# Sixteen decoder entries on one core: eight in flight instead of seven, with fewer tiles for each

## The chip, the core and the metric

The kernel runs on one core of a Trainium2 chip. The core has four engines that compute: TensorE (PE in the profile, with its weight loads as PEld), VectorE (DVE), ScalarE (ACT) and GpSimd (POOL). SyncE (SP) issues most DMA transfers. Each engine works through its own list of instructions in order and waits on semaphores for the others. Products are written to PSUM, which has eight banks; everything else lies in SBUF. The metric is the time of one launch on the device in microseconds.

## What is computed

Sixteen independent entries (batch 16) of 128 tokens by 256 features pass through a decoder of two layers, all in float32. Each of the six blocks adds its output to x and normalises:

```
L0 attn : q,k,v = x W; q,k,v -> latents of 32; rotary; softmax (causal); back to 256; W
L0 xattn: linear attention with the context: q (k^T v); layer norm with gamma, beta
L0 ffn  : FP4 grid of x and of the weights; silu(gate) * up; FP4 grid again; down
L1 attn : softmax (causal) y, plus a moving part: sum_j qa.ka (x[j+1] - y[j]); W
L1 xattn: softmax with a mask over the context; W; norm; relu MLP 256-1024-256; norm
L1 ffn  : FP6 grid of x and of the weight; W + bias
```

In each attention there are 16 heads of 16 features. "FP4 grid" means that each block of 16 values is scaled by its largest and rounded to a grid of few values; FP6 has blocks of 32.

## The kernel before, in words

One entry fits the array: 128 tokens on the 128 partitions. An entry is written as a Python generator, `stages` (it calls `l0_attn` L837, `l0_xattn` L894, `l0_ffn` L985, `l1_attn` L1027, `l1_xattn` L1113 and `l1_ffn` L1176). Each `yield` names what the next step needs: the engine on which it starts, a resource ("p": one of four general PSUM banks; "quad": the one set of four banks for scores; "e": a pair of tiles for exponentials), and the tiles that it reads. Three more generators prepare weights: `fold_values` makes one matrix for the values of the first attention (resource "wv"), `later_biases` and `quantised_weights` (resource "gu").

A planner at the end of the kernel runs all generators when the program is built. It keeps its own clock for each engine, takes the step that can start first, and writes its instructions into the engines' lists. So the order of all instructions is fixed before the launch. Where several steps could start within 0.05 us of the first, it prefers one that holds a PSUM bank or another tile just written, then the one that became ready in the earliest interval of 8 us (each entry is shifted by its number in the table `DELAY`), then the oldest entry. `NS` (L18) entries are in flight. Entry b takes place b mod NS and starts when the entry before it in this place is done; the last place is given away only when the quantised weights are ready, since they are prepared in its tiles.

If the planner foresees that PE will wait at least `LEAST` us (L25), it fills the share `SHARE` of the gap with filler products (`fill`, L147; `ps_filler` in the profile), which nobody reads, as long as two of the general banks are free.

Every place owns tiles of SBUF, which `mine` (L252) gives out: A, B, C, D for intermediate results, v for values, mr for the mask's terms, yT for transposed features and results of 256 columns, and two tiles x0_ and x1_, between which x (`new_x`, L515) and the transposed input of the next entry (`load_input`, L278) take turns. A new use of a tile waits for all reads of the old one. `features` (L685) transposes a tile through PE and copies it with ACT into yT; `out_proj` (L691) multiplies, adds bias and residual, and writes the sum into yT. The tile bd, for the block diagonal in `l0_xattn`, is one for all entries.

The first attention computes scaled queries (`ps_qfk`, written to q in tile B) and then the values (`ps_v`). An attention takes scores in the quad (`ps_s`), their maxima on DVE (`nm`), splits them on POOL into three bfloat16 terms, transposes those on PE (`ps_tm`), computes transposed scores less the maxima (`ps_st`), exponentials on ACT (`e`), the causal zeros on POOL, the product with the values (`ps_yp`), and transposes that back (`ps_ty`). Masked parts of the score matrices and the small products of 16 features use 32-row groups of the array, all other products the whole array.

Of the kernel before, what the change touches and what calls it, by code (L numbers as in the profile page):

```python
# [16 lines left out]
P = 128  # L17
NS = 7  # L18
W3 = 3 * 4
# [4 lines left out]
EPS = 1e-5  # L24
SHARE, LEAST = 0.75, 0.8  # L25

DELAY = (3.07, 2.06, 3.48, 0.32, 3.35, 1.80, 2.92, 0.82, 1.65, 1.28, 1.58, 3.49, 2.27, 4.62, 2.80, 1.07, 0.06)
WINDOW = 3.413
# [185 lines left out]
def decoder_kernel(ctx: ExitStack, tc: tile.TileContext, a: dict, out: bass.AP):  # L214
# [12 lines left out]

    turns = {}

    def turn(name, n):  # L230
        turns[name] = turns.get(name, -1) + 1
        return turns[name] % n

    rings = {}
# [17 lines left out]
    def mine(s, tag, shape, name, dtype=F32):  # L252

        return ring(own, f"{tag}{s}", 1, shape, dtype, name)
# [23 lines left out]
    def load_input(b):  # L278

        s = b % NS  # L280
        t = mine(s, f"x{turn(f'x{s}', 2)}_", [P, 2, P], f"xT_in_{b}")
        nc.sync.dma_start(out=t, in_=a["xT"][:, :, b * T : (b + 1) * T])
        if b < 3:
            clock.load(t, 8 * P)
        else:
            arrives(t)
        incoming[b] = t
# [86 lines left out]
    for i in range(0, 5, 2):  # L374
        n = min(2, 5 - i)
        cm = wk.tile([P, 2, 64], F32, tag="bd", name="cm", bufs=1)
        GP.memset(cm, 0.0)
        GP.affine_select(
            out=cm, in_=cm, compare_op=ALU.is_ge, fill=-1e30, base=96 - 64 * i, pattern=[[-64, 2], [-1, 64]],
            channel_multiplier=1,  # L380
        )
        GP.tensor_copy(causal[:, i : i + n, :], cm[:, :n, :])
# [41 lines left out]
    clock.load(rows, 4 * (NROW - NADD))  # L424
    l2o = own.tile([P, H * VW], F32, tag="B5", name="l2o")
    nc.gpsimd.dma_start(out=l2o, in_=a["rows"][:, ROW["l2o"]].partition_broadcast(P))
# [17 lines left out]
    def bank(shape, name, dtype=F32):  # L444
        return psum(ps_p, "p", shape, name, dtype)
# [71 lines left out]
    def new_x(b, s, name):  # L517

        k = turn(f"x{s}", 2)
        return mine(s, f"x{k}_", [P, D], f"x_{name}_{b}")  # L520

# [162 lines left out]

    def features(y, s, name):  # L685

        yT = mine(s, "yT", [P, 2, P], f"yT_{name}")
        yield from transposed(y, 2, yT, name)
        return yT

    def out_proj(yT, weight, bias, residual, s, name):  # L691

        yield "PE", "p", yT
        p = bank((D,), f"op_{name}")
        product(p, yT, weight, bias)
        yield "V", p
        h = mine(s, "yT", [P, D], f"h_{name}")
        V.tensor_tensor(h, p, residual, ALU.add)
        return h
# [55 lines left out]
    def fold_values():  # L755
# [5 lines left out]
        yield "S", t  # L761
        vT = own.tile([P, 4, P], F32, tag="B4", name="fold_vT")
        S.copy(vT, t)
# [3 lines left out]
        yield "S", t  # L767
        kT = own.tile([P, P], F32, tag="D4", name="fold_kT")
        S.copy(kT, t)
# [4 lines left out]

        m = own.tile([P, 8 * VW], F32, tag="A4", name="fold_md")
        GP.memset(m, 0.0)
# [60 lines left out]
    def l0_attn(b, s):  # L837
# [12 lines left out]
        sin = w["sinT"].unsqueeze(1).to_broadcast([P, 4, P])  # L850
        q = mine(s, "B", [P, 4, P], f"q0_{b}")
        k = mine(s, "C", [P, 4, P], f"k0_{b}")
# [13 lines left out]
        for j, dst in ((0, rot), (2, k)):  # L866
# [5 lines left out]
            GP.tensor_tensor(dst, ro[0], ro[1], ALU.add)  # L872
        yield "PE", "p", rot
        p = bank((4, P), f"qfk_{b}")
        PE.matmul(p, lhsT=w["w_wqk"], rhs=rot, start=True, stop=True)
        yield "S", p
        S.activation(q, p, AF.Identity, bias=wqk_b, scale=LAT**-0.5)
        ctx_ = context(b, s, "0")
        yield "PE", "p", "wv", xT
# [3 lines left out]
        v = values(s, f"a0_{b}")  # L883
        S.copy(v[:, : H * VW], p)
        y = yield from attention(b, s, q, k, v, None, f"a0_{b}", "A")
        yield "PE", "bt", y
        yT = yield from features(y, s, f"a0_{b}")
        h = yield from out_proj(yT, w["w_cproj"], "cproj", xs[b], s, f"a0_{b}")
        xs[b] = new_x(b, s, "a0")
# [4 lines left out]
    def l0_xattn(b, s, ctx_):  # L894
        yield "PE", "p", ctx_
        p = bank((2 * D,), f"x0kv_{b}")
        product(p, ctx_, w["w_x0kv"], "x0kv")
        kv = mine(s, "A", [P, 2 * D], f"kv_{b}")
        yield "S", p
        S.copy(kv, p)  # L900
        xT = yield from features(xs[b], s, f"x0_{b}")
        yield "PE", "p2", kv, xT
        p2 = bank((2, P), f"x0m_{b}")
        for c in range(2):
            PE.matmul(
                p2[:, c, :], lhsT=kv[:, c * P : (c + 1) * P], rhs=kv[:, D + c * P : D + (c + 1) * P],
                start=True, stop=True,
            )
        p = bank((2, P), f"x0q_{b}")
        project(p, w["w_x0q"], xT)  # L910
        yield "S", p, p2
        qT = mine(s, "B", [P, 2, P], f"x0q_{b}")
        biased(qT, p, cols[:, COL["x0q"]])
        yield "V", "bd", p2
        bd = work("bd", 1, [P, 2, P], f"bd_{b}")
        V.tensor_tensor(bd, p2, w["blk"].unsqueeze(1).to_broadcast([P, 2, P]), ALU.mult)
        yield "PE", "p", bd, qT
        p3 = bank((2, P), f"x0a_{b}")
        for c in range(2):
            PE.matmul(p3[:, c, :], lhsT=qT[:, c, :], rhs=bd[:, c, :], start=True, stop=True)  # L920
        yield "V", p3
        h = mine(s, "yT", [P, D], f"h_x0_{b}")
        V.tensor_tensor(h, p3.rearrange("p a b -> p (a b)"), xs[b], ALU.add)
        xb = with_bias(b, s, "x0b", "A")
        z = mine(s, "C", [P, D], f"z_x0_{b}")
        yield from layernorm_affine(z, h, "x0g", xb, f"x0i_{b}")
        xs[b] = new_x(b, s, "x0")
        yield from layernorm(xs[b], z, f"x0_{b}")

# [55 lines left out]
    def l0_ffn(b, s):  # L985
        yield "V", "gu", xs[b]
        q = mine(s, "D", [P, D], f"xq_{b}")
        yield from fp4(q, xs[b], D, f"x_{b}")
        qT = yield from features(q, s, f"xq_{b}")
        h = mine(s, "A", [P, FF], f"hh_{b}")  # L990
# [29 lines left out]
        yield "V", p  # L1020
        r = mine(s, "yT", [P, D], f"h_f0_{b}")
        V.tensor_tensor(r, p, xs[b], ALU.add)
# [4 lines left out]
    def l1_attn(b, s):  # L1027
        xT = yield from features(xs[b], s, f"x1a_{b}")
        sc = HD**-0.5
        q = mine(s, "B", [P, 2, P], f"a1q_{b}")  # L1030
        k = mine(s, "C", [P, 4, P], f"a1k_{b}")
        qa = mine(s, "A", [P, 2, P], f"a1qa_{b}")
        ka = mine(s, "D", [P, 4, P], f"a1ka_{b}")
        yield "PE", "p", xT
# [9 lines left out]
        p = bank((2, P), f"a1k2_{b}")  # L1044
        project(p, w["w_a1k2"], xT)
        yield "S", p
        biased(ka[:, 2:4, :], p, dense_col("a1k2"), AF.Tanh, sc * 0.01)
# [9 lines left out]
        GP.tensor_copy(v3[:, :, :HD], xs[b].rearrange("p (h d) -> p h d", d=HD))  # L1057
        ahead = mine(s, "yT", [P, D], f"ahead_{b}")
        nc.sync.dma_start(out=ahead[: P - 1, :], in_=xs[b][1:P, :])
# [44 lines left out]
        yield "S", p  # L1104
        yT = mine(s, "yT", [P, 2, P], f"yT_a1_{b}")
        S.copy(yT, p)
        h = yield from out_proj(yT, w["w_a1p"], "a1p", xs[b], s, f"a1_{b}")
        xs[b] = new_x(b, s, "a1")
# [4 lines left out]
    def l1_xattn(b, s, ctx_):  # L1113
# [24 lines left out]
        S.copy(v[:, : H * VW], p)  # L1138
        xT = yield from features(xs[b], s, f"x1_{b}")
        yield "PE", "p", xT  # L1140
# [4 lines left out]
        y = yield from attention(b, s, q, k, v, mr, f"x1_{b}", "A")  # L1145
        yT = yield from features(y, s, f"x1y_{b}")
        h = yield from out_proj(yT, w["w_x1o"], "x1o", xs[b], s, f"x1_{b}")
        t = mine(s, "C", [P, D], f"x1_{b}")
        yield from layernorm_affine(t, h, "g1", row("be1"), f"x1i_{b}")
        tT = yield from features(t, s, f"x1t_{b}")  # L1150
        ff = []
# [15 lines left out]
        yield "V", p  # L1167
        h = mine(s, "yT", [P, D], f"h_ff_{b}")
        V.tensor_tensor(h, p, t, ALU.add)
# [6 lines left out]
    def l1_ffn(b, s):  # L1176
# [4 lines left out]
        yield from fp6(q, xs[b], D, f"f1_{b}")  # L1181
        qT = yield from features(q, s, f"f1_{b}")
        h = yield from out_proj(qT, wf, "f1", xs[b], s, f"f1_{b}")
        y = mine(s, "C", [P, D], f"out_{b}")
# [14 lines left out]
    places = {"quad": ("s", 1), "p": ("p", 1), "p2": ("p", 2), "t2": ("t2", 1), "t22": ("t2", 2)}  # L1199
    places.update((tag, (tag, 1)) for tag in ("fc", "fC", "silu", "bd", "mT", "mi", "mb"))  # L1200
    free = {"e": [0.0, 0.0], "mx": [0.0, 0.0], "gu": [], "wv": [], "bt": []}
# [79 lines left out]
    while runs:  # L1281
# [3 lines left out]


        at, _, run = min(
            (r for r in able if r[0] <= first + 0.05),
            key=lambda r: (not r[2].held, round((r[2].ready + DELAY[int(r[1]) if r[1] >= 0 else B]) / 8.0), r[1]),
        )  # L1290
        run.step(at)
# [118 lines left out]
```

## Time and profile before

| | us |
|---|---|
| median of three runs | 985.59 (984.91 to 986.45) |
| the profiled execution, its own time | 988.3 |
| its span, first to last instruction | 986.6 |
| PE busy | 919.7 |
| of it fillers (182) | 44.5 |
| PEld busy | 723.2 |
| DVE busy | 700.7 |
| ACT busy | 508.8 |
| POOL busy | 432.2 |

The mean granted clock of TensorE is 0.983 of full speed. The DMA engines are nearly idle after the first 50 us. Since almost all operations pass through one helper, nearly every line in the profile is L208 and operations are told apart by their tiles. A name such as `ps_op_a` is that of a PSUM tile: op for output product, the suffix for the block (a: an attention, x: a cross attention, f: a feed-forward block). Busy times of PE are modelled at their ends and include short stalls between pipelined products.

### The profile page before, as it was taken

The numbers are of one execution on the slowest core, as the hardware profiler recorded it, in microseconds if no ns is written. First come the engines' busy times: TensorE is split into PE (matmuls) and PEld (weight loads), VectorE is DVE, ScalarE is ACT, GpSimd is POOL, SyncE is SP. The second block draws the span as 40 slices with busy tenths as digits, with TensorE's granted clock in tenths as the row PEclk, the third lists the DMA queues.
The fourth block names the chain that finished last, engine by engine and source line by source line (L and its number), as shares of the span: only waits on it lengthen the run. The fifth ranks groups of instructions, "written<-read, shape, count | busy, mean of one in ns | idle before, by whom it ended". The sixth has DMA issues, their size and how long they took to land.

```text
span 986.6 us, 28364 instructions
## 1 busy us (share of the span) xinstructions
PE 919.7 (93%) x11965; PEld 723.2 (73%) x11965; DVE 700.7 (71%) x1440; ACT 508.8 (52%) x1113; POOL 432.2 (44%) x898
## 2 busy tenths in 40 slices
PE   7889899999899999999999999999998899999996
PEld 6566567777678878788777787878776687686764
DVE  5999999976764666659596967957666458963544
ACT  3244445665556444655546666555555545555432
POOL 3335523644435344445363464435434435344321
PEclk9899999999999989999999999999999999999998
DMA  8910000000000000000000000000000000000000
GB/s 230 210 45 7 28 7 7 11 9 20 5 23 12 19 25 21 23 22 17 18 18 16 21 13 7 24 1 23 21 13 25 8 11 7 14 13 15 10 7 12
DMA packets 47864, 25.57 MB, mean 26 GB/s; under 512 B 23004, under 2 KB 45516, under 8 KB 47480
## 3 DMA queue, kind: packets, MB, share of 16 engines
q1 hardware_dynamic: 46816, 22.39, 8.3%
q8 instruction: 94, 1.54, 0.6%
q0 software_dynamic: 192, 0.93, 0.4%
q10 hardware_dynamic: 728, 0.44, 0.1%
q14 instruction: 34, 0.28, 0.1%
HBM read 19.57 MB, written 2.10 MB: 22 GB/s over the span
## 4 chain that ended last, share of the span: by engine, by line
PE 55%; DVE 26%; ACT 8%; POOL 6%; issue 4%; DMA 0%; ACTq 0%; POOLq 0%; DVEq 0%
PE ps_ff L208 10%; PE ps_s_a L208 3%; PE ps_dn L208 3%; PE ps_st_a L208 3%; DVE nm_a L208 3%; DVE rope L208 2%; PE ps_op_a L208 2%; PE ps_x0kv L208 2%; PE ps_pg L208 2%; PE ps_pu L208 2%; PE ps_a1qk L208 2%; PE ps_yt L208 2%; DVE hh L208 2%; PE ps_qk L208 2%; PE ps_st_x L208 2%
## 5 line engine op out<-in xcount | busy, mean ns | idle before, releaser
L208 POOL TENSOR_SCALAR_AFFINE_SELECT e_a<-e_a 128x1024 f32<-128x1024 f32 x64 | 76.0, 1190 | 88.9 <-ACT e_a L208 88.7
L208 DVE TENSOR_REDUCE nm_a<-ps_s_a 128x16 f32<-128x2048 f32 x32 | 73.1, 2286 | 28.4 <-PE ps_s_a L208 28.2
L208 ACT ACTIVATE e_a<-ps_st_a 128x1024 f32<-128x1024 f32 x64 | 65.7, 1030 | 27.1 <-PE ps_st_a L208 26.9
L208 PE MATMUL ps_ff<-yT_x1t,w 128*128 128x128 f32 x512 | 63.1, 277 | 1.0 <-ACT yT_x1t L208 1.0
L208 PEld LDWEIGHTS ps_ff<-yT_x1t,w 128*128 128x128 f32 x512 | 60.1, 192 | 4.4 <-issue 2.1
L208 PE MATMUL ps_ff<-w,ff 128*128 128x256 f32 x256 | 61.0, 381 | 0.0
L208 ACT ACT_TABLE_LOAD x41 | 52.6, 1283 | 12.8 <-DMA brow<-in_rows_dram 9.0
L208 POOL CAST maxima<-nm_a 128x16 bf16<-128x16 f32 x32 | 8.9, 279 | 98.8 <-DVE nm_a L208 98.8
L208 PEld LDWEIGHTS ps_ff<-w,ff 128*128 128x128 f32 x256 | 46.2, 190 | 7.7 <-ACT ff L208 1.0
L208 ACT ACTIVATE ff<-ps_ff,cols 128x128 f32<-128x128 f32 x128 | 36.5, 369 | 27.1 <-PE ps_ff L208 27.0
L208 PE MATMUL ps_dn<-qw_down,hT 128*128 128x256 f32 x192 | 47.2, 383 | 0.7 <-ACT hT L208 0.5
L208 PE MATMUL ps_pg<-gu,yT_xq 128*128 128x352 f32 x128 | 44.7, 471 | 0.7 <-DVE hh L208 0.4
L208 DVE TENSOR_REDUCE nm_x<-ps_s_x 128x16 f32<-128x2048 f32 x16 | 36.5, 2282 | 11.4 <-PE ps_s_x L208 11.1
L161 PE MATMUL ps_filler<-ones,ident_b 128*128 128x512 bf16 x182 | 44.5, 383 | 0.0
L208 PE MATMUL ps_pu<-gu,yT_xq 128*128 128x352 f32 x128 | 43.2, 460 | 0.6 <-DVE bd L208 0.6
L208 PE MATMUL ps_yp_a<-e_a,v_a 128*32 128x128 f32 x1024 | 36.5, 281 | 3.6 <-POOL e_a L208 2.3
L208 ACT ACTIVATE e_x<-ps_st_x 128x1024 f32<-128x1024 f32 x32 | 31.8, 1026 | 13.7 <-PE ps_st_x L208 13.7
L208 PEld LDWEIGHTS ps_dn<-qw_down,hT 128*128 128x128 f32 x192 | 34.4, 190 | 5.6 <-ACT hT L208 0.7
L208 POOL TENSOR_SCALAR_AFFINE_SELECT maT<-maT 128x1024 f32<-128x1024 f32 x16 | 18.0, 1123 | 42.0 <-ACT maT L208 42.0
L208 ACT ACTIVATE x_x<-z_x,rstd_x 128x256 f32<-128x256 f32 x32 | 19.3, 604 | 31.7 <-POOL rstd_x L208 26.8
L208 ACT ACTIVATE x_a<-h_a,rstd_a 128x256 f32<-128x256 f32 x32 | 19.4, 605 | 31.4 <-POOL rstd_a L208 29.9
L208 PEld LDWEIGHTS ps_yp_a<-e_a,v_a 128*32 128x32 f32 x1024 | 26.3, 111 | 12.0 <-issue 4.8
(367 smaller groups left out, 2659.2 us busy)
## 6 DMA issues: line engine op xcount, KB each, us to landing
ctx<-in_ctxT_dram SPq DMA_DIRECT2D x32, 128.0 KB
xT_in<-in_xT_dram SPq DMA_DIRECT2D x16, 128.0 KB
w<-in_w_dram SPq DMA_DIRECT2D x2, 1024.0 KB
x_in<-in_x_dram SPq DMA_DIRECT2D x16, 128.0 KB
out_dram<-out SPq DMA_DIRECT2D x16, 128.0 KB
ahead<-x_f SPq DMA_DIRECT2D x16, 127.0 KB
mi<-in_mask_dram SPq DMA_DIRECT2D x16, 64.0 KB
rows<-in_rows_dram POOLq DMA_DIRECT2D x1, 768.0 KB, 5.5
```

What stands on the lines that cost most here:

```text
L161: self._e.matmul(bank, lhsT=lhsT, rhs=rhs, start=True, stop=True)
L208: return f(*args, **kw)
```

## The change

- Eight entries are in flight (`NS` 8). Sixteen entries are so two rounds.
- To make room, each place loses yT and one of its two x tiles. What went to yT goes to one of A, B, C, D whose content the entry has done with; the place is now an argument of `features` and `out_proj`. x has one tile, x, written in place by each norm. The next entry's transposed input goes to B. bd goes to the entry's own D. The row-shifted x ("ahead") shares tile A with the rectified queries qa.
- In the first attention the values' product stands ahead of the scaled queries, since the transposed input lies in B, where the queries go.
- The planner's rule is shorter: of the steps that can start first, without the margin of 0.05 us, the one that became ready first, then the oldest entry. `DELAY` and the preference for held tiles go. `LEAST` is 1.0 instead of 0.8 us.
- In the preparation, some tiles of places 4 and 5 are taken from other tiles or places.

```
-NS = 7
+NS = 8
-SHARE, LEAST = 0.75, 0.8
-
-DELAY = (3.07, 2.06, 3.48, 0.32, 3.35, 1.80, 2.92, 0.82, 1.65, 1.28, 1.58, 3.49, 2.27, 4.62, 2.80, 1.07, 0.06)
+SHARE, LEAST = 0.75, 1.0
...
-        t = mine(s, f"x{turn(f'x{s}', 2)}_", [P, 2, P], f"xT_in_{b}")
+        t = mine(s, "B", [P, 2, P], f"xT_in_{b}")
...
-        k = turn(f"x{s}", 2)
-        return mine(s, f"x{k}_", [P, D], f"x_{name}_{b}")
+        return mine(s, "x", [P, D], f"x_{name}_{b}")
...
-    def features(y, s, name):
+    def features(y, s, at, name):
 
-        yT = mine(s, "yT", [P, 2, P], f"yT_{name}")
+        yT = mine(s, at, [P, 2, P], f"yT_{name}")
...
-    def out_proj(yT, weight, bias, residual, s, name):
+    def out_proj(yT, weight, bias, residual, s, at, name):
...
-        h = mine(s, "yT", [P, D], f"h_{name}")
+        h = mine(s, at, [P, D], f"h_{name}")
...
-        yield "PE", "p", rot
-        p = bank((4, P), f"qfk_{b}")
-        PE.matmul(p, lhsT=w["w_wqk"], rhs=rot, start=True, stop=True)
-        yield "S", p
-        S.activation(q, p, AF.Identity, bias=wqk_b, scale=LAT**-0.5)
-        ctx_ = context(b, s, "0")
         yield "PE", "p", "wv", xT
         p = bank((H * VW,), f"v0_{b}")
         product(p, xT, wv, "l2o")
         yield "S", p
         v = values(s, f"a0_{b}")
         S.copy(v[:, : H * VW], p)
+        yield "PE", "p", rot
+        p = bank((4, P), f"qfk_{b}")
+        PE.matmul(p, lhsT=w["w_wqk"], rhs=rot, start=True, stop=True)
+        q = mine(s, "B", [P, 4, P], f"q0_{b}")
+        ctx_ = context(b, s, "0")
+        yield "S", p
+        S.activation(q, p, AF.Identity, bias=wqk_b, scale=LAT**-0.5)
...
-        yield "V", "bd", p2
-        bd = work("bd", 1, [P, 2, P], f"bd_{b}")
+        yield "V", p2
+        bd = mine(s, "D", [P, 2, P], f"bd_{b}")
...
-        qa = mine(s, "A", [P, 2, P], f"a1qa_{b}")
-        ka = mine(s, "D", [P, 4, P], f"a1ka_{b}")
+        both = mine(s, "A", [P, 4, P], f"a1qa_{b}")
+        qa, ahead = both[:, 0:2, :], both[:, 2:4, :].rearrange("p a b -> p (a b)")
...
-
-        at, _, run = min(
-            (r for r in able if r[0] <= first + 0.05),
-            key=lambda r: (not r[2].held, round((r[2].ready + DELAY[int(r[1]) if r[1] >= 0 else B]) / 8.0), r[1]),
-        )
+        at, _, run = min((r for r in able if r[0] <= first), key=lambda r: (r[2].ready, r[1]))
```

More of the change, by code (lines that the diff above doesn't have):

```diff
@@ L226, in decoder_kernel @@
     ps_p = ctx.enter_context(tc.tile_pool(name="ps_p", bufs=4, space=bass.MemoryType.PSUM))
[L228 to L232, printed above, removed]
     rings = {}
@@ L375, in decoder_kernel @@
         n = min(2, 5 - i)
-        cm = wk.tile([P, 2, 64], F32, tag="bd", name="cm", bufs=1)
+        cm = wk.tile([P, 2, 64], F32, tag="mb", name="cm", bufs=2)
         GP.memset(cm, 0.0)
@@ L424, in decoder_kernel @@
     clock.load(rows, 4 * (NROW - NADD))
-    l2o = own.tile([P, H * VW], F32, tag="B5", name="l2o")
+    l2o = own.tile([P, H * VW], F32, tag="D5", name="l2o")
     nc.gpsimd.dma_start(out=l2o, in_=a["rows"][:, ROW["l2o"]].partition_broadcast(P))
@@ L761, in fold_values @@
         yield "S", t
-        vT = own.tile([P, 4, P], F32, tag="B4", name="fold_vT")
+        vT = own.tile([P, 4, P], F32, tag="C6", name="fold_vT")
         S.copy(vT, t)
@@ L767, in fold_values @@
         yield "S", t
-        kT = own.tile([P, P], F32, tag="D4", name="fold_kT")
+        kT = own.tile([P, P], F32, tag="D6", name="fold_kT")
         S.copy(kT, t)
@@ L773, in fold_values @@
         yield "S", p
-        m = own.tile([P, 8 * VW], F32, tag="A4", name="fold_md")
+        m = own.tile([P, 8 * VW], F32, tag="A6", name="fold_md")
         GP.memset(m, 0.0)
@@ L850, in l0_attn @@
         sin = w["sinT"].unsqueeze(1).to_broadcast([P, 4, P])
-        q = mine(s, "B", [P, 4, P], f"q0_{b}")
         k = mine(s, "C", [P, 4, P], f"k0_{b}")
@@ L884, in l0_attn @@
         S.copy(v[:, : H * VW], p)
+        yield "PE", "p", rot
[5 more added lines that the diff above has]
+        S.activation(q, p, AF.Identity, bias=wqk_b, scale=LAT**-0.5)
         y = yield from attention(b, s, q, k, v, None, f"a0_{b}", "A")
         yield "PE", "bt", y
-        yT = yield from features(y, s, f"a0_{b}")
-        h = yield from out_proj(yT, w["w_cproj"], "cproj", xs[b], s, f"a0_{b}")
+        yT = yield from features(y, s, "B", f"a0_{b}")
+        h = yield from out_proj(yT, w["w_cproj"], "cproj", xs[b], s, "C", f"a0_{b}")
         xs[b] = new_x(b, s, "a0")
@@ L900, in l0_xattn @@
         S.copy(kv, p)
-        xT = yield from features(xs[b], s, f"x0_{b}")
+        xT = yield from features(xs[b], s, "C", f"x0_{b}")
         yield "PE", "p2", kv, xT
@@ L921, in l0_xattn @@
         yield "V", p3
-        h = mine(s, "yT", [P, D], f"h_x0_{b}")
+        h = mine(s, "C", [P, D], f"h_x0_{b}")
         V.tensor_tensor(h, p3.rearrange("p a b -> p (a b)"), xs[b], ALU.add)
         xb = with_bias(b, s, "x0b", "A")
-        z = mine(s, "C", [P, D], f"z_x0_{b}")
+        z = mine(s, "D", [P, D], f"z_x0_{b}")
         yield from layernorm_affine(z, h, "x0g", xb, f"x0i_{b}")
@@ L988, in l0_ffn @@
         yield from fp4(q, xs[b], D, f"x_{b}")
-        qT = yield from features(q, s, f"xq_{b}")
+        qT = yield from features(q, s, "B", f"xq_{b}")
         h = mine(s, "A", [P, FF], f"hh_{b}")
@@ L1020, in l0_ffn @@
         yield "V", p
-        r = mine(s, "yT", [P, D], f"h_f0_{b}")
+        r = mine(s, "D", [P, D], f"h_f0_{b}")
         V.tensor_tensor(r, p, xs[b], ALU.add)
@@ L1027, in l1_attn @@
     def l1_attn(b, s):
-        xT = yield from features(xs[b], s, f"x1a_{b}")
+        xT = yield from features(xs[b], s, "D", f"x1a_{b}")
         sc = HD**-0.5
@@ L1045, in l1_attn @@
         project(p, w["w_a1k2"], xT)
+        ka = mine(s, "D", [P, 4, P], f"a1ka_{b}")
         yield "S", p
@@ L1057, in l1_attn @@
         GP.tensor_copy(v3[:, :, :HD], xs[b].rearrange("p (h d) -> p h d", d=HD))
-        ahead = mine(s, "yT", [P, D], f"ahead_{b}")
         nc.sync.dma_start(out=ahead[: P - 1, :], in_=xs[b][1:P, :])
@@ L1104, in l1_attn @@
         yield "S", p
-        yT = mine(s, "yT", [P, 2, P], f"yT_a1_{b}")
+        yT = mine(s, "A", [P, 2, P], f"yT_a1_{b}")
         S.copy(yT, p)
-        h = yield from out_proj(yT, w["w_a1p"], "a1p", xs[b], s, f"a1_{b}")
+        h = yield from out_proj(yT, w["w_a1p"], "a1p", xs[b], s, "B", f"a1_{b}")
         xs[b] = new_x(b, s, "a1")
@@ L1138, in l1_xattn @@
         S.copy(v[:, : H * VW], p)
-        xT = yield from features(xs[b], s, f"x1_{b}")
+        xT = yield from features(xs[b], s, "A", f"x1_{b}")
         yield "PE", "p", xT
@@ L1145, in l1_xattn @@
         y = yield from attention(b, s, q, k, v, mr, f"x1_{b}", "A")
-        yT = yield from features(y, s, f"x1y_{b}")
-        h = yield from out_proj(yT, w["w_x1o"], "x1o", xs[b], s, f"x1_{b}")
+        yT = yield from features(y, s, "B", f"x1y_{b}")
+        h = yield from out_proj(yT, w["w_x1o"], "x1o", xs[b], s, "D", f"x1_{b}")
         t = mine(s, "C", [P, D], f"x1_{b}")
         yield from layernorm_affine(t, h, "g1", row("be1"), f"x1i_{b}")
-        tT = yield from features(t, s, f"x1t_{b}")
+        tT = yield from features(t, s, "B", f"x1t_{b}")
         ff = []
@@ L1167, in l1_xattn @@
         yield "V", p
-        h = mine(s, "yT", [P, D], f"h_ff_{b}")
+        h = mine(s, "A", [P, D], f"h_ff_{b}")
         V.tensor_tensor(h, p, t, ALU.add)
@@ L1181, in l1_ffn @@
         yield from fp6(q, xs[b], D, f"f1_{b}")
-        qT = yield from features(q, s, f"f1_{b}")
-        h = yield from out_proj(qT, wf, "f1", xs[b], s, f"f1_{b}")
+        qT = yield from features(q, s, "A", f"f1_{b}")
+        h = yield from out_proj(qT, wf, "f1", xs[b], s, "D", f"f1_{b}")
         y = mine(s, "C", [P, D], f"out_{b}")
@@ L1199, in decoder_kernel @@
     places = {"quad": ("s", 1), "p": ("p", 1), "p2": ("p", 2), "t2": ("t2", 1), "t22": ("t2", 2)}
-    places.update((tag, (tag, 1)) for tag in ("fc", "fC", "silu", "bd", "mT", "mi", "mb"))
+    places.update((tag, (tag, 1)) for tag in ("fc", "fC", "silu", "mT", "mi", "mb"))
     free = {"e": [0.0, 0.0], "mx": [0.0, 0.0], "gu": [], "wv": [], "bt": []}
```

## The prediction

> **What bounds the kernel now.** I read the page's busy shares and its 40 slices first.
>
> ```profile
> PE 919.7 (93%) x11965; PEld 723.2 (73%) x11965; DVE 700.7 (71%) x1440; ACT 508.8 (52%) x1113; POOL 432.2 (44%) x898
> ...
> PE   7889899999899999999999999999998899999996
> ...
> PEclk9899999999999989999999999999999999999998
> ```
>
> TensorE is the bound: 93%, and no other engine over 71%. But part of its work is fillers, products that nobody reads. So I took the stretches next, for all instructions and then for the fillers alone.
>
> ```profile
> 0.00:200.00 200.00, 178.22 (x2212) 131.57 (x2212) 179.60 (x364) 85.72 (x193) 88.00 (x179) 0.97 0.26 67
> 200.00:880.00 680.00, 649.99 (x8671) 523.56 (x8659) 473.07 (x973) 379.98 (x825) 310.42 (x641) 0.99 0.06 16
> 880.00:986.60 106.60, 91.48 (x1094) 68.06 (x1094) 48.06 (x105) 43.12 (x97) 33.77 (x80) 0.97 0.04 12
> ```
>
> ```profile
> 0.00:200.00 200.00, 17.87 (x71) 0.97 0.26 67
> 200.00:880.00 680.00, 6.82 (x27) 0.99 0.06 16
> 880.00:986.60 106.60, 19.78 (x84) 0.97 0.04 12
> ```
>
> Columns: stretch, length, then busy us of PE, PEld, DVE, ACT, POOL (in the second view PE's fillers alone), clock, DMA. Useful PE work is busy less fillers: 643.2 us of 680 in the middle (94.6%), 71.7 of 106.6 in the tail (67%). The first 200 us are DVE's (179.6), quantising weights. The tail's timeline shows the loss itself:
>
> ```profile
> 956.42 2.97 PE L161 MATMUL ps_filler<-ones,ident_b 128*128 128x512 bf16 x13
> ...
> 969.29 6.64 PE L161 MATMUL ps_filler<-ones,ident_b 128*128 128x512 bf16 x30
> 978.55 0.41 PE L208 MATMUL ps_tr_f<-ident,f1q 128*128 128x128 f32 x2 [2.62 <-DVE f1q L208]
> ```
>
> From 969.29 on PE only waits for the last entry's layer norm and FP6 grid, fillers or not. The third loss is the clock, here around 348 us:
>
> ```profile
> 346.10:349.50 3.40, 1.61 (x11) 0.95 (x14) 3.26 (x6) 1.81 (x4) 2.93 (x6) 1.00 0.05 15
> 349.50:352.90 3.40, 3.40 (x54) 2.89 (x55) 2.20 (x4) 0.72 (x2) 2.14 (x3) 0.50 0.06 19
> 352.90:356.30 3.40, 3.40 (x40) 2.45 (x43) 1.03 (x3) 1.59 (x2) 0.43 (x2) 0.50 0.03 8
> ```
>
> A window in which PE is about half busy is followed by one or two at half clock. The middle has four such windows (one at 236.9, two here, one at 752.3): 4 x 3.4 us at half speed, 6.8 us of work lost.
>
> **The change, part by part.** No instruction of the computation is added or removed; the order is new. I compared the two orders of PE instructions as the programs write them.
>
> *Fillers.* 182 before, 97 after. Up to the same point of the work, about 200 us: 71 before, 69 after. In the middle 27 before, none after. In the tail 84 before, 28 after (4 and 24, ahead of the last two entries' FP6 transposes). The planner fills three quarters of a gap it foresees, so it foresees no gap of 1 us or more in the middle. The raised threshold explains little: only two of the 28 groups before have two fillers, the size that it forbids.
>
> *The tail.* With 7 in flight, 16 entries run as 7, 7 and 2: the last 180 of 6978 product instructions before belong to entries 14 and 15 alone. In the new order, 8 and 8, entries 11 to 15 are all in those 180. What stays is the last chain: 17.3 us (986.6 - 969.29), six fillers fewer (6 x 0.221 = 1.3; 30 took 6.64), plus the gap of 4 fillers (4 x 0.221 / 0.75 = 1.2): 17.2 us, with 1.6 of useful work in it. The other 70.1 us (71.7 - 1.6) now run like the middle.
>
> *The middle's share p.* Taking out the 27 fillers alone gives 643.2 / (680 - 6.8) = 95.5%. I also take back half of the clock loss, 3.4 us, since no large gap is foreseen: 643.2 / 669.8 = 96.0%. Bounds are from the 100 us stretches, fillers out: the best is 600 to 700 (98.19 - 0.81 = 97.4%), the worst 700 to 800 (92.30 - 1.46 = 90.8%). I lean to the upper half because dependent steps lie farther apart. I summed the PE work that the order puts between two steps of one entry, at the spacing of such products in the trace. Medians: values' product to its transposes in the last attention 1.9 us before, 4.2 after; transposed maxima to the second scores there 2.4 and 9.8; scores to maxima 4.8 and 7.8. Before, the 1.9 us are just enough: at 948.32 that product starts, and its transposes at 951.22 without idle time behind one step of another entry.
>
> *Dearer switches of the array's mode.* Between row groups and the full array I count 373 changes before, 392 after. Starts of full-array products follow each other in 112 ns; across a change 200 to 309 ns. So 19 x about 0.145 = 2.7 us (1.7 to 3.7).
>
> The page "TensorEngine Tiling (Array Packing)", section Key Properties, says that a change of tiling mode, though not of tile, drains TensorE; this speaks against an order that alternates more. It gives no price; the spacings above are such a drain, and a sum by the rule alone could not be made.
>
> *Values' product ahead of scaled queries.* Attention now waits for one more PE step and one ACT step behind the values: ps_qfk 0.59 x 2 passes, overlapping to 1.0, and ACT q 0.69. Later seven other entries cover it; for the first entry, behind the folded weights, I take 1.0 (0 to 1.7). The copy of the values is ahead of q on ACT now; nobody but this entry waits.
>
> *Tiles.* One x tile: the layer norm's write (0.60 us on ACT) must follow all reads of the old x, of which only "ahead", the DMA of x moved one row, is not on the entry's own chain. It is issued before the attention that precedes the write, ten steps earlier; the output's subtraction waits for it in both kernels. Bounds 0 to 0.7 (its issue takes 670 ns) a time, I take 0. It now lands in the second half of the tile that holds the rectified queries, whose reader, the masked product, comes after attention: 0. The next entry's xT goes to tile B and is issued at the same place, its x after the place is free: x is read only at the first residual, some 1000 PE instructions later. Features and results in tiles A to D replace yT; each overwrites what an earlier step of the same chain has read: 0. Tile bd, one for all before, becomes the entry's own, which can only free DVE (0.4 us each): 0. POOL's bias sum xb_be (0.85 us) now has to follow the reads of t's transposed copy, done before the ACT step that precedes it: 0. On SP's queue the contexts' loads wait for PE as before (111.9 us behind ps_qfk, off the path); what stands behind them is loads for much later. If that cover went, a load would cost its whole landing to one entry of eight, not to PE.
>
> *ACT.* 31 table loads instead of 41, 1.28 us each: 12.8 us of an engine that is 52% busy; 0, bounds -1 and 0.
>
> **Sum.** Start 200 - 0.5 (two fillers) = 199.5; modes and queries 3.7; useful work of middle and tail 643.2 + 70.1 = 713.3 at share p; end 17.2. So time = 220.4 + 713.3 / p. At p = 96.0%: 220.4 + 743.0 = 963.4 against the profiled span of 986.6, that is -23.2. The profiled run took 988.3, the median of the three runs shown is 985.6, 1.0 below the span; so 962.4, say 962.
>
> The skill's first page, "Trainium Kernel Development and Optimization", section Performance Expectations, calls matmul busy time a poor measure because products are pipelined, and points to weight-load busy. By that measure the tail's useful loads are 68.06 - 8.01 = 60.1 us, about 58.7 before the last chain, at the middle's (523.56 - 2.48) / 680 = 76.6%: 76.6 us instead of the 73.0 that 70.1 takes at 96.0%, so 966 by it. The rule also makes the 96% less of a ceiling than it looks.
>
> **Rivals.**
>
> A. *The middle stays or gets a little worse.* New stalls of under 1 us, which get no filler, take the freed time; a first-ready rule also lets started steps hold PSUM banks longer, and with fewer than two of four free no filler is put in, so missing fillers don't prove missing gaps. For it: 200 to 300 us had 90.6% useful (93.72 - 3.13), seven points below the best stretch. Against: the longer covers. At 94.6%: 974.4 - 1.0 = 973; it spans p from 95.3% to 93.4%, 968 to 983.
>
> B. *Slower: bank starvation in the middle.* Eight entries queue for the four general PSUM banks and the one quad of score banks; PE stops until ACT or DVE has read a bank, windows fall to half busy, and the clock halves after them. It decides from p = 93.1% down (713.3 / 0.931 = 766.2, and 766.2 + 220.4 = 986.6). Two of seven middle stretches lie below that already; at the worst one's 90.8% the time is 1005. Against: the stretches from 300 to 500 ran seven entries at 97%.
>
> C. *Much better.* Busy shares hide small stalls, and longer covers remove them and all four slow windows. At 97.4%: 952.7 - 1.0 = 952; at the best stretch's whole busy share, 98.2%, 946.
>
> D. *The tail's gain is not real:* the last five entries collide on DVE (FP6 grid, some 4 us each with norms) and the tail stays at 67%. That gives back 70.1 / 0.67 - 73.0 = 32 us, 994. Against: DVE is 45% busy in the tail (48.06 of 106.6). I put it with B.
>
> **How the numbers follow.** Forecast, p 95.3 to 96.8%, 956 to 968: 0.49. A: 0.23. C: 0.13. B and D: 0.12. Within 0.2% (2 us), about what a measurement of this kernel tells from no change: 0.03. Faster: 0.49 + 0.23 + 0.13 = 0.85. The range leaves out B and D, and the lower half of C: 947 to 983.
>
> **What would show it.** Right: ps_filler x97, none between 200 and 930 us; 880 us to the end over 80% useful; useful share of the middle 95.3% or more; clock mean above 0.983; the last filler group of 24 followed by one FP6 transpose. Wrong: PE waits for ACT or DVE copies growing in the middle, with half-clock windows there; a share under 93.1%; a first pair of gate and up products much later than 127 us, which would mean that first-ready order delays the weights.

## The result, and the profile after

The changed kernel takes 969.87 us (median of four runs, 968.28 to 972.29) against 986.02 before: a ratio of 0.984, 95% interval 0.982 to 0.986. It is 1.6% faster. The prediction said 962 with a range of 947 to 983. The profiled execution took 968.28, its span is 966.2, which stands against 963.4 in the prediction's sum.

The page of the changed kernel, busy shares and slices:

```profile
PE 896.6 (93%) x11880; PEld 715.2 (74%) x11880; DVE 699.8 (72%) x1440; ACT 491.4 (51%) x1103; POOL 437.1 (45%) x898
...
PE   7888899888999999999999999999998899999996
...
PEclk9998999999999999999999999999999999999998
```

The share of PE is again 93%, though the time fell: a share of busy time alone would not have shown the gain. The stretches do, first all instructions, then the fillers alone (columns as in the prediction: stretch, length, busy us of PE, PEld, DVE, ACT, POOL, clock, DMA):

```profile
0.00:200.00 200.00, 167.82 (x2140) 122.51 (x2140) 163.77 (x320) 82.47 (x177) 80.86 (x158) 0.95 0.27 69
200.00:880.00 680.00, 653.47 (x8991) 531.00 (x8992) 482.48 (x976) 372.18 (x833) 325.61 (x668) 1.00 0.06 16
880.00:966.20 86.20, 75.30 (x751) 61.67 (x749) 53.54 (x145) 36.70 (x95) 30.68 (x73) 0.95 0.03 11
```

```profile
0.00:200.00 200.00, 16.59 (x69) 0.95 0.27 69
200.00:880.00 680.00, 0.00 (x0) 1.00 0.06 16
880.00:966.20 86.20, 6.37 (x28) 0.95 0.03 11
```

Busy less fillers, the useful work, is 151.2 us in the first 200 us (before: 160.3), 653.5 of 680 in the middle, 96.1% (before 94.6%), and 68.9 of 86.2 in the tail, 80% (before 67%). So the middle and the tail gained, and the start lost 9.1 us. The tail in time order:

```profile
946.57 1.03 PE L159 MATMUL ps_filler<-ones,ident_b 128*128 128x512 bf16 x4
947.80 0.44 PE L206 MATMUL ps_tr_f<-ident,f1q 128*128 128x128 f32 x2 [0.21 <-DVE f1q L206]
...
949.67 5.34 PE L159 MATMUL ps_filler<-ones,ident_b 128*128 128x512 bf16 x24
957.10 0.56 PE L206 MATMUL ps_tr_f<-ident,f1q 128*128 128x128 f32 x2 [2.09 <-DVE f1q L206]
```

On PE only the last entry's chain is left then, 16.5 us from 949.67 to the end. Six entries write their results after 880 us (from 901.26 to 962.84), before four (from 883.89 to 983.26). Between 200 us and that point PE does this:

```profile
200.00:949.67 749.67, 720.58 (x9710) 588.94 (x9710) 530.02 (x1103) 406.30 (x923) 353.10 (x732) 1.00 0.05 15
949.67:966.20 16.53, 8.19 (x32) 3.73 (x30) 5.99 (x18) 2.59 (x5) 3.18 (x9) 0.73 0.05 16
```

With the four fillers (0.9 us) out, that is 719.7 / 749.67 = 96.0% useful.

### The profile page after: what moved, and what is told of

Same layout as the page of the kernel before. It is cut to its first block, busy times and chain, and to the rows that moved or that the text cites. A ratio compares the mean times of both kernels' runs of the same rounds, so it can differ in the third digit from the quotient of the medians.

```text
span 966.2 us, 28159 instructions
## 1 busy us (share of the span) xinstructions
PE 896.6 (93%) x11880; PEld 715.2 (74%) x11880; DVE 699.8 (72%) x1440; ACT 491.4 (51%) x1103; POOL 437.1 (45%) x898
## 5 line engine op out<-in xcount | busy, mean ns | idle before, releaser
L206 POOL TENSOR_SCALAR_AFFINE_SELECT e_a<-e_a 128x1024 f32<-128x1024 f32 x64 | 76.6, 1197 | 55.1 <-ACT e_a L206 54.9
L206 POOL CAST maxima<-nm_a 128x16 bf16<-128x16 f32 x32 | 10.8, 336 | 89.6 <-DVE nm_a L206 89.6
L206 POOL TENSOR_TENSOR rot<-rope,rope 128x512 f32<-128x512 f32 x16 | 21.6, 1350 | 37.1 <-DVE rope L206 35.2
L206 PE MATMUL ps_qk<-xT_in,w_qkv 128*128 128x128 f32 x256 | 36.1, 305 | 1.3 <-DMA xT_in<-in_xT_dram 0.7
L206 PEld LDWEIGHTS ps_qk<-xT_in,w_qkv 128*128 128x128 f32 x256 | 34.6, 218 | 2.6 <-ACT yT_x L206 0.9
L206 POOL TENSOR_TENSOR k<-rope,rope 128x512 f32<-128x512 f32 x16 | 21.9, 1368 | 29.6 <-DVE rope L206 29.6
## 6 DMA issues: line engine op xcount, KB each, us to landing
a1qa<-x_f SPq DMA_DIRECT2D x16, 127.0 KB
```

What stands on the lines that cost most here:

```text
L206: return f(*args, **kw)
```

## The experiments

Twelve kernels were run, each in three rounds beside the kernel before on the same chip; ratios are to that. The parts of the change form a table: entries in flight, tiles (with the values' place), and the planner's rule. "Table" is the shift `DELAY`, whose numbers are those of the kernel before in every row that has it. Start is useful PE work in the first 200 us, middle the useful share from 200 to 880 us.

| kernel | in flight | tiles | rule | median us | ratio (95%) | start us | middle |
|---|---|---|---|---|---|---|---|
| before | 7 | old | old, table | 986.0 | 1 | 160.3 | 94.6% |
| e11 | 7 | old | old, no table | 1006.90 | 1.022 (1.018 to 1.026) | 154.0 | 92.5% |
| e2 | 7 | old | new | 1028.57 | 1.045 (1.042 to 1.047) | 155.0 | 93.2% |
| e10 | 7 | new | old, table | 1019.17 | 1.034 (1.031 to 1.036) | 153.3 | 91.2% |
| e12 | 7 | new | old, no table | 1015.84 | 1.030 (1.027 to 1.034) | 156.4 | 93.0% |
| e3 | 7 | new | new | 1016.28 | 1.032 (1.030 to 1.035) | 155.6 | 94.2% |
| e1 | 8 | new | old, table | 979.72 | 0.995 (0.993 to 0.997) | 157.0 | 95.5% |
| after | 8 | new | new | 969.87 | 0.984 (0.982 to 0.986) | 151.2 | 96.1% |
| e4 | 8 | new, queries first | new | 963.90 | 0.978 (0.975 to 0.981) | 153.0 | 95.9% |
| e5 | 8 | new | old in preparation, then new | 959.12 | 0.974 (0.970 to 0.977) | 159.5 | 96.2% |
| e6 | 8 | new, queries first | as e5 | 979.28 | 0.993 (0.990 to 0.995) | 154.2 | 94.1% |
| e7 | 8 | new, no fillers | new | 977.12 | 0.991 (0.988 to 0.993) | 158.3 | 95.4% |
| e13 | 8 | new | as e5, margin kept | 956.02 | 0.968 (0.964 to 0.972) | 158.6 | 96.7% |
| e14 | 8 | new | as e5, 4 us intervals | 961.06 | 0.975 (0.972 to 0.978) | 158.6 | 95.8% |

### One part alone, or one undone

The first four asked which part makes the gain and which the loss at the start. The rule alone, on the kernel before:

```
-            (r for r in able if r[0] <= first + 0.05),
-            key=lambda r: (not r[2].held, round((r[2].ready + DELAY[...]) / 8.0), r[1]),
+        at, _, run = min((r for r in able if r[0] <= first), key=lambda r: (r[2].ready, r[1]))
```

> The kernel before with only the planner's rule of the change (first able, then first ready; fillers from 1.0 us), seven in flight, all tiles as before. Theory 1, the gain is the eighth entry: no gain here; the order writes 228 fillers instead of 182, 46 more at 0.244 us, so about 986 + 11 = 997 us, with the tail after 880 us still under 70% useful. Rival 2, the gain is the shorter rule: 975 us or less.

It took 1028.57 us, 4.5% slower: theory 1 in direction, but four times the 11 us that its fillers foretold. Then the changed kernel with one entry fewer:

```
-NS = 8
+NS = 7
-        vT = own.tile([P, 4, P], F32, tag="C6", name="fold_vT")
+        vT = own.tile([P, 4, P], F32, tag="C4", name="fold_vT")
(kT and m likewise)
```

> The changed kernel with seven entries in flight instead of eight; tiles, values ahead of queries and rule as changed (three tiles of the preparation go to place 4). Theory 1: the gain is lost, 222 fillers instead of 97, 125 more at 0.244 us, 970 + 30 = 1000 us, between 990 and 1005. Rival 2, rule or tiles give the gain: 975 us or less. Against e2 it prices the tiles and the values' place alone: theory 1 expects less than 4 us between the two.

1016.28 us, 11 above theory 1's range. This run and the changed kernel differ in the number of entries alone (beside the places of three preparation tiles), so under these tiles and this rule the eighth entry is worth 46.4 us. The same step under the old rule with its table (e10 to e1 below, which differ in the filler threshold too) is worth about 39 us, so it is not the luck of one pair of orders. Its stretches and fillers show where the time goes:

```profile
200.00:880.00 680.00, 650.97 (x8836) 527.82 (x8838) 460.38 (x943) 367.66 (x818) 306.73 (x644) 0.99 0.06 16
880.00:1014.90 134.90, 109.31 (x1097) 76.19 (x1094) 65.16 (x149) 47.61 (x107) 38.01 (x87) 0.98 0.03 10
```

```profile
200.00:880.00 680.00, 10.22 (x42) 0.99 0.06 16
880.00:1014.90 134.90, 27.41 (x117) 0.98 0.03 10
```

The tail is 48.7 us longer than the changed kernel's, with 81.9 useful us in 134.9 (61%). The last three results are written at 900.66, 1003.51 and 1011.52, so for 114 us only two entries are left (before: for 49 us, from 937.37 on). The middle is at 94.2% instead of 96.1%. The other prediction in this expectation failed: e2 and e3 differ by 12 us, not by less than 4, and the new tiles are on the faster side.

The changed kernel with the old rule:

```
-        at, _, run = min((r for r in able if r[0] <= first), key=lambda r: (r[2].ready, r[1]))
+            (r for r in able if r[0] <= first + 0.05),
+            key=lambda r: (not r[2].held, round((r[2].ready + DELAY[...]) / 8.0), r[1]),
```

> The changed kernel with the rule of before (margin 0.05 us, held tiles first, DELAY and intervals of 8 us), eight in flight, fillers from 1.0 us. Theory 3, the 9 us that the changed kernel loses in its first 200 us come from the first-ready rule, which lets entries pass the preparation of weights: useful PE work in 0 to 200 us returns from 151 to about 160 us, the tail is longer (fillers in the last part 57 instead of 28, 7 us), in sum 965 to 972. Rival 4, the loss at the start comes from eight entries or from the values' place: useful work of the start stays near 151 and the time is 975 or more.

979.72 us, above theory 3's range and above the 975 of rival 4. Its start goes part of the way that theory 3 says, 157.0 useful us instead of 151.2, where it said about 160. The tail (68.2 useful of 98.5, 13.2 us of fillers) and the middle (95.5%) cost more than that. With eight entries the new rule is 10 us better as a whole and worse at the start; the old one ran here with a table made for seven.

Scaled queries first, as before:

```
+        q = mine(s, "A", [P, 4, P], f"q0_{b}")       (queries' product and copy moved up)
         yield "PE", "p", "wv", xT
-        q = mine(s, "B", [P, 4, P], f"q0_{b}")
-        y = yield from attention(b, s, q, k, v, None, f"a0_{b}", "A")
+        y = yield from attention(b, s, q, k, v, None, f"a0_{b}", "B")
```

> The changed kernel with the scaled queries ahead of the values again (queries in tile A, attention's result in B, its features in A). Rival 4, values first costs the start: useful work in 0 to 200 us rises from 151 to 157 us or more, and the time falls to 964 or less. Theory 3, it costs about nothing: within 4 us of the changed kernel; the order writes 123 fillers instead of 97, so rather 970 + 26 x 0.244 = 976.

963.90 us: 6 us less, against theory 3, in spite of 26 more fillers. But the start rose by 1.8 us only, not by the 6 that rival 4 asked for. So neither account fits; that was followed up in e6.

### The start, the fillers, and the tiles

The old rule during the preparation of the weights only:

```
+        if any(r.age == 0.5 for r in runs):      (quantised_weights still running)
+            at, _, run = min((r for r in able if r[0] <= first + 0.05),
+                key=lambda r: (not r[2].held, round(r[2].ready / 8.0), r[1]))
+        else:
             at, _, run = min((r for r in able if r[0] <= first), key=lambda r: (r[2].ready, r[1]))
```

> The changed kernel, with the rule of before (margin, held tiles first, intervals of 8 us, without the table DELAY) only while the weights are being prepared, and the first-ready rule afterwards. Theory 3, first-ready order costs the start and only the start: useful PE work in 0 to 200 us returns from 151 to 157, as with the old rule throughout, the middle keeps 96%, and the time falls by the 6 us that this is worth: 964, between 961 and 967. Rival 5, what the start gains is given back later because entries leave it less evenly: 968 or more.

959.12 us. The start as the stretches and fillers of this run show it:

```profile
0.00:200.00 200.00, 169.33 (x2140) 127.69 (x2144) 168.59 (x331) 87.21 (x190) 83.01 (x160) 0.95 0.27 69
```

```profile
0.00:200.00 200.00, 9.84 (x41) 0.95 0.27 69
```

159.5 useful us, 8.3 more than in the changed kernel, at the same mean clock, and the middle keeps 96.2%. The time falls by 10.8 us, a little more than theory 3 expected. With eight in flight and the values first, the loss at the start is the first-ready rule's, and it is not given back later. At seven in flight it is not: there the start is 153 to 156 us under either rule (e2, e3, e10, e11, e12), and only the kernel before, with its table, reaches 160.3.

> The same with the scaled queries ahead of the values as well. If the two causes at the start add up: 958 to 961 us. If they are one and the same delay of the first entries: as one of them alone, 963 to 966.

This joined e5 and e4, both of which had gained. It took 979.28 us, outside both expectations and 20 us above e5. The start fell back to 154.2, 5.3 us less useful work than in e5, and the middle loses more:

```profile
200.00:880.00 680.00, 642.26 (x8887) 519.90 (x8878) 469.56 (x949) 371.94 (x809) 313.90 (x655) 0.99 0.05 16
```

Less 2.7 of fillers, 94.1% useful against e5's 96.2%, some 15 us less; yet its order has 95 fillers, e5's 91. So the planner did not foresee this loss. The 6 us of e4 can't be called the price of the values' place: with the other rule in the preparation the same move costs 20 us. What it is worth by itself stays open. The same holds for the rule: with the queries first, the old rule in the preparation adds 1.2 us of useful work to the start (153.0 to 154.2) and costs 15 us of time (e4 to e6).

No fillers (the threshold set out of reach, `LEAST = 1e9`):

> The changed kernel without any filler product (the threshold is never reached). Theory: the 97 fillers keep the clock up at the start and the end and cost no time of their own, since they stand in gaps; without them more windows there run at half clock: 2 to 4 windows more, each worth up to 1.7 us: 971 to 977. Rival: they delay real work behind them, by the planner's errors; then the kernel gets faster without, 966 or less.

977.12 us, 7 us more, at the upper end of what the theory expected. The start:

```profile
0.00:200.00 200.00, 158.32 (x2092) 120.25 (x2093) 161.20 (x323) 81.56 (x173) 81.42 (x157) 0.87 0.27 69
```

The clock is 0.87 there instead of 0.95, and 0.956 over the run instead of 0.983. (The 158.3 busy us are at a slower clock, so they are not more work: in the changed kernel the two products `ps_qfk` take 1.02 us at 84.5 us and 1.69 at 95.7, at half clock.) The clock is lower without fillers in all four executions (0.956 to 0.969, against 0.978 to 0.988 in the changed kernel). What the fillers alone are worth in time is not shown: the order of this kernel is another from 34 us on, since the planner's clock counts the fillers, and another order alone moves the time by some 10 us here (e1 and e5 against the changed kernel). The rival, that the kernel gets faster without them, did not come.

> Seven in flight with the rule, DELAY and threshold of before, but the tiles and the values' place of the change: the price of these alone. Theory 1: within 10 us of before, rather slower, since the table DELAY was made for another order: 986 to 995 (216 fillers instead of 182, 34 x 0.244 = 8 us). Rival 2, the tiles by themselves free the order: 975 or less, which would take away from the eighth entry what I give to it.

Seven in flight, the old rule with its table, and the new tiles: 1019.17 us, 33 us above before and outside theory 1. Either the tiles cost 33 us or the table fits one program only. Two runs told these apart. The table taken out of the kernel before (` + DELAY[...]` removed from the key):

> The kernel before without the table DELAY (all shifts zero), nothing else changed. Theory 6: the table is fitted to this one program, and its order is some 30 us better than an ordinary order at seven in flight; without it 1010 to 1030, like the other three orders with seven (1016, 1019, 1029). Rival 7: the table is worth little and the changed tiles cost 33 us at seven in flight: 985 to 995.

1006.90 us, 3 under the range of theory 6 but far from rival 7: in the old tiles the table is worth 21 us. And the same with the new tiles:

> Seven in flight, tiles and values' place of the change, rule and threshold of before, no table: with e11 the price of the tiles alone. Theory 6: within 12 us of e11, either way. Rival 7: 20 us or more above e11.

1015.84 us. The new tiles and the values' place cost 9 us at seven in flight under this rule, as theory 6 allowed. With the table of another program they cost 3 more.

### A faster version

> As e5 (old rule while the weights are prepared), and the margin of 0.05 us kept in the rule afterwards; the order has 76 fillers, e5 91. If fewer foreseen gaps mean less time: 955 to 958. If orders that close differ by more than the plan tells: anywhere from 956 to 980.

e5 with the margin of 0.05 us kept in the later rule (`r[0] <= first + 0.05`): 956.02 us, a ratio of 0.968, the lowest median of all, in the range expected of fewer fillers; 658 of 680 us in the middle, 96.7%, and no filler there. Its interval (0.964 to 0.972) overlaps those of e5 and e14, so the margin's 3 us are not clear of noise.

> As e5 with intervals of 4 instead of 8 us during the preparation; 91 fillers as e5. If e5's gain is a property of its rule: 956 to 963. If it is the luck of one order: 966 or more.

961.06 us. Three kernels with the old rule in the preparation and values first give 956 to 961. e5 and e13 share their order up to about 407 us, e14's leaves e5's at about 70 us; so with the values first this gain is not the luck of one order, but e6 shows that it does not carry over to the queries first. Against both kernels e13 is the version to keep: 3.2% under before, 1.6% under the change.

## Why the prediction was right, and where it was off

**The eighth entry.** The part of the argument that carried the forecast holds. Six entries share the stretch after 880 us instead of four, the last chain is 16.5 us (forecast 16.0, and 1.2 for the four fillers before it), and the middle's useful share is 96.0% up to 949.67, the p of the forecast to the digit. The time itself, 969.87, lies in the stretch given to rival A (968 to 983), not in the forecast's own 956 to 968, and the gain is 16.2 us where 23 were forecast; but A's mechanism did not come, since the middle got better, and what lies between is in the start and in the step from span to median. Rival A's 94.6%, rival B's 93.1% and rival D's collision on DVE did not come; DVE is 62% busy in the tail (53.54 of 86.2) and PE 80% useful.

**The start was mis-sized.** The step "Start 200 - 0.5 (two fillers) = 199.5; modes and queries 3.7" took the same number of fillers (71 and 69) for the same start. At 200 us 9.1 us of useful work are missing, which take 9.5 us at 96%: 209.5 instead of 203.2, 6.3 us more. The other terms give 3.5 back, 0.7 in the last chain and 2.8 since 2.7 us less useful work were left than this counts, so the sum missed the span by 2.8. The last line of the prediction's "what would show it" named a delay of the weights; but the first silu starts at 132.0 instead of 127.0 us only. A part of the loss is in waits such as these, in windows of 3.4 us of the changed kernel:

```profile
86.80:90.20 3.40, 0.60 (x4) 0.31 (x3) 3.33 (x5) 0.77 (x3) 1.51 (x1) 1.00 0.14 39
90.20:93.60 3.40, 2.87 (x68) 2.54 (x69) 3.26 (x8) 0.34 (x1) 1.32 (x2) 0.51 0.02 5
93.60:97.00 3.40, 3.40 (x9) 2.10 (x9) 3.33 (x7) 0.39 (x1) 2.04 (x2) 0.50 0.00 0
107.30:110.70 3.40, 0.98 (x7) 0.83 (x8) 3.17 (x7) 1.78 (x3) 0.95 (x1) 1.00 0.03 7
110.70:114.10 3.40, 3.35 (x54) 2.35 (x57) 3.17 (x7) 0.02 (x1) 1.22 (x1) 0.50 0.14 39
```

DVE is busy throughout (3.2 to 3.3 of 3.4) and PE waits, in the first window for DVE's block of the down weight (2.62 us), in the fourth for another block (1.68) and for exponentials on ACT (1.05), and works at half clock after each. At 100 us the changed kernel is 6.8 us of useful busy time behind. But at 140 us it is 1.3 behind only (6.8 us more than before were at half clock by then, so up to 3.4 us of work must be added), and 7.8 of the 9.1 us come after that, at full clock and without fillers, in these two stretches, first of the kernel before, then of the changed one:

```profile
140.00:160.00 20.00, 20.00 (x198) 13.81 (x196) 19.45 (x36) 10.01 (x19) 6.53 (x10) 1.00 0.03 8
180.00:200.00 20.00, 20.00 (x266) 15.88 (x264) 18.54 (x38) 10.83 (x27) 13.18 (x33) 1.00 0.05 15
```

```profile
140.00:160.00 20.00, 16.28 (x204) 11.70 (x208) 19.48 (x39) 10.63 (x19) 8.00 (x8) 1.00 0.03 8
180.00:200.00 20.00, 15.85 (x114) 10.72 (x112) 9.00 (x26) 10.79 (x24) 7.08 (x19) 1.00 0.02 5
```

In the first DVE is as busy as before, in the second it stands idle half the time as well, so waiting for DVE is not the whole account. Runs e1 and e5 show that for this kernel, eight in flight and values first, the rule in this stretch is the cause; e4 and e6 show that with the queries first it is not. Which of its three parts (margin, held tiles, intervals) does it was not separated.

**The clock.** "I take back half of the clock loss" in the middle: one half-clock window of 3.4 us is left there (at 728.5 us) instead of four, so more came back. With three of four taken back, 5.1 us, the prediction's sum would have given a share of 96.3%, so that 96.0 came out to the digit is in part luck. "Clock mean above 0.983" was wrong: it is 0.983 again, since the start has 20.4 us at half clock (before 13.6) and the end 9.0 (before 5.6). The prediction's reading, that a window in which PE is about half busy is followed by half clock, holds for the windows it showed and not for all (see the last section).

**The median.** I placed the median 1.0 under the span, as before. It lies 3.7 above it: the profiled execution was the fastest of its four, 1.6 under the median, and its own time is 2.1 above its span. This step, not the sum, is 4.7 of the 7.5 us between 962.4 and 969.87.

**The tiles.** "Each overwrites what an earlier step of the same chain has read: 0" was not measured wait by wait, but e11 and e12 put the tiles and the values' place at 9 us in seven. The forecast did not suffer, since it was read from the whole new order, not from the parts. For the same reason it did not need to know what the runs then showed: the change throws away a fitted table (21 us) and adds these 9, and the eighth entry, worth 46 in its own tiles, has to pay for both. 986 + 21 + 9 + 0 (e12 to e3, the rule with its threshold) - 46 gives the 970. This is one path through the table, and the prices hold on it alone: in the old tiles the rule costs 22 us (e11 to e2), and under the new rule the tiles gain 12 (e2 to e3).

**Two readings of the fillers.** The count of fillers foretold the direction of the change and of e2, e3 and e10, but not the sizes: e2 has 46 more than before and is 43 us slower, not 11. In e4 the direction failed too: 26 more than the changed kernel, and 6 us faster. And between orders that differ little in fillers (e5, e6: 91, 95) the time differs by 20 us. The weight-load reading of the prediction, which gave 966 for the median, came nearer to it than 962; that is accident, since it assumed 76.6% for the loads and the stretch to 949.67 has 78%.

## What to carry to other kernels

When independent entries run several at a time on a bound engine, try a number in flight that divides the number of entries. After 880 us PE had 35 to 59 us without useful work in the six kernels with seven in flight, and 15 to 30 in the eight with eight; the step from e3 to the changed kernel won 46 us, some 36 of them there and 13 in the middle, less what the start lost. Only seven and eight were run, so even rounds and one more entry are not told apart. Read the gain from useful work by stretch (busy less fillers), since the share of busy time was 93% in both kernels. A fitted order can be worth its gain for one program only: the table won 21 us in the program that it was made for and cost 3 with the new tiles, so price the change against the unfitted kernel too, or a good change looks smaller than it is. Try a rule of its own for the preparation of shared weights, and measure it in the order you keep: here it won 9 to 11 us with the values first (e14, e5) and lost 15 with the queries first (e4 to e6).

## What was not expected of the hardware

The clock halved after windows in which PE was only partly busy: in the changed kernel after 0.60 and after 0.98 us of 3.40, and before after 1.61. The Trainium skill's page "TensorE: Matmul & The Clock Gate", section What's actually happening, gives the throttled state after at least one idle window of about 3.4 us; here windows busy for a fifth to a half of their time went ahead of it, and the measurement decides. But not every such window is followed by half clock. Here are two of the changed kernel that are not, each with the window behind it:

```profile
223.30:226.70 3.40, 1.48 (x7) 0.95 (x6) 3.30 (x6) 1.39 (x3) 1.78 (x2) 1.00 0.02 5
226.70:230.10 3.40, 2.81 (x21) 2.71 (x22) 2.08 (x5) 0.63 (x2) 0.71 (x2) 1.00 0.00 0
312.10:315.50 3.40, 1.73 (x10) 1.37 (x9) 1.30 (x2) 3.35 (x6) 0.67 (x1) 1.00 0.08 26
315.50:318.90 3.40, 3.40 (x25) 2.97 (x23) 3.26 (x8) 1.77 (x3) 1.94 (x2) 1.00 0.00 1
```

In the kernel before, one with 1.85 us (at 503.1) was not, and one with 2.21 (at 233.5) was. So the busy share in the profile does not tell it by itself, and no threshold comes out of these runs. Without fillers the mean clock fell from 0.983 to 0.956; the 7 us that this kernel is slower are not the clock's alone, since its order differs too.
